# Expert stage of a two-layer fp32 kernel: stationary expert weights taken from a copy made by ScalarE, with the routing slots, two norms and the final sums rearranged

## The chip, the cores and the metric

The kernel runs on one core of a Trainium2 chip. The time is device microseconds (us) of that core for one execution; three runs of the kernel before took 1727.71, 1731.00 and 1731.02 us, so the median is 1731.0 us. One more execution was recorded by the hardware profiler. Engines are named as in the profile: PE is TensorE's matmul side, PEld its weight loads, DVE VectorE, ACT ScalarE, POOL GpSimd, SP the engine that issues most DMAs.

## The reference, cut to what matters

The program is two transformer layers over 4 x 512 tokens of width 256, all in float32. Layer 0 is a decayed linear attention and a gated feed-forward with Hadamard rotations. Layer 1 is an attention with 16 heads, then a second attention with 32 query and 8 key heads of width 64, and behind it a mixture of 16 experts of which each token takes 4. The change is mostly in the mixture:

```python
x = x + o @ wo
h = _rms(x, ff_ln_w)
logits = h @ wg
topv, topi = jax.lax.top_k(logits, TOP_K)
gate = jax.nn.softmax(topv, -1)
weights = jnp.zeros_like(logits).at[bidx, sidx, topi].set(gate)
a = jax.nn.silu(jnp.einsum('bsd,edh->bseh', h, w1)) * jnp.einsum('bsd,edh->bseh', h, w3)
y = jnp.einsum('bseh,ehd->bsed', a, w2)
moe = jnp.einsum('bsed,bse->bsd', y, weights)
return x + moe
```

Here d and h are both 256. The kernel computes only the four chosen experts of each token.

## The kernel before, in words

The kernel is written in stages, and in the stages spoken of here the order of work on each engine is the order of the program text (`manual_schedule`): each engine takes its instructions in that order, and waits on semaphores where data or a buffer is not ready. "Tile n" below is a group of 128 token rows of one expert.

**Layer 0 attention** (lines 657 to 685) walks over 16 groups of 128 tokens, and puts three or so pieces of the next batch's projections (`pieces_of`) into each step.

**Second attention of layer 1** (lines 1859 to 1950) walks over 16 units u, each in five slots f. Beside the attention itself, each slot calls `extras`, which takes pieces from three lists: the norms, and the routing of the batch before. `route(b)` is the routing of batch b, some 20 pieces and 16 scatters: squares, root, scale, the logits, the ranks of the 16 experts, gates, places in the experts' lists (`places`, 28 short matmuls), `choose` (the row numbers), and 16 scatters by POOL that write the tokens' rows into a DRAM list `xs`. After `route(2)` come `plan_tiles(0)` (four pieces) and `read_plan(0)`, which turn the counts into a list of tiles: for each of 79 tiles, where its rows start, where its expert's weights lie, how many rows are real. A call `extras(plain, banked, scatters)` lets that many pieces of each kind go; a "pause" ends a slot's plain pieces. `norms` (line 1081) makes the inverse deviations for the two norms in three pieces; its `begin` holds a DVE operation and the two ACT operations behind it.

**Expert stage** (lines 1955 to 2114). 79 tiles of 128 rows; the first 33 (`NFIRST`) need only the first three batches. `route(3)` and the second plan run inside this stage, two pieces an iteration. The weights of the experts in use lie in SBUF as `wall`, 1536 columns an expert (w1 and w3 in halves of the inner dimension, 1024 columns, then w2 in 512), fetched by 16 DMAs of 768 KB; a matmul finds its expert by a register address (`w_at`). For tile i:

- `fetch_rows(i)`: one DMA of 128 rows from `xs` into `xin`.
- `turn_in(i)`: two PE transposes of `xin` into PSUM (`ptx`), DVE copies them to `hTx`; three small DVE operations make the gate and the row numbers to which the tile goes (`goes`).
- `hidden(i)`: two matmuls with `hTx` stationary and 512 columns of `wall` moving, so that rows lie on partitions: `ph`. ACT makes `gx` = silu of the first half, DVE multiplies by the second half: `ax`.
- `turn_hidden(i)`: two PE transposes of `ax` into PSUM (`pa`), ACT copies them to `aTx`.
- `give(i)`: two matmuls with `aTx` stationary and 256 columns of `wall` moving: `pyx`. ACT scales by the gate (`yx`), and POOL adds the rows to one of two DRAM accumulators by an indirect DMA (`acc`, even tiles to one, odd tiles to the other).

A float32 matmul shows as two instructions on PE, so `hidden` is four of 512 columns and `give` four of 256. Line 1986 is the helper that issues both, so they are told apart by tile names. Iteration n of the loop holds, in this order: `hidden(n+1)`, the weights' DMA for place n+2, `address(n+2)`, `turn_in(n+2)`, `turn_hidden(n)`, `give(n-1)`, `fetch_rows(n+3)`, and two pieces of routing.

**End** (lines 2097 to 2114). For each batch, SP reads both accumulators, DVE adds them and the residual `xt`, and SP writes the result. Tile 78, the last, adds to the even accumulator.

## Time and profile before

| What | Value |
|---|---|
| median of three runs | 1731.0 us |
| profiled execution: its own time | 1726.86 us |
| profiled execution: span of the page | 1725.1 us |
| mean granted PE clock | 0.963 of full |
| PE, PEld busy | 1620.5 us (94%), 941.9 us (55%) |
| DVE, ACT, POOL busy | 1028.1, 825.9, 897.1 us |
| DMA over the span | 146.23 MB, 79 GB/s from and to HBM |
| second attention, by its first and last output projection | 733 to 1408 us |
| first transpose of a tile's rows, last `yx` | 1414.5 us, 1698.5 us |

A line of the profile's timeline gives the start in us, the length in us, the engine, the line of the kernel, the operation, the tile written and the tiles read, and in brackets how long the engine had been idle and what released it. Lines of a table by stretches give, for PE, PEld, DVE, ACT and POOL, the busy us and in brackets the number of instructions, then the granted PE clock (1.00 is full), the DMA engines' share and GB/s. Ends of matmuls are modelled; starts are recorded, so the pace of PE is read from starts.

### The profile page before, as it was taken

The page shows a single profiled execution, that of the slowest core. Times are in us where ns is not written, and L with a number is a line of the kernel's source. Part 1 is how long each engine was busy: PE and PEld are TensorE (multiplying, and loading weights), DVE is VectorE, ACT ScalarE, POOL GpSimd, SP SyncE. Part 2 cuts the span into 40 slices and gives each one's busy share as a digit, 9 for nine tenths or more (in the row PEclk, how much of TensorE's full clock was granted, in tenths as well). Part 3 has the DMA queues.
Part 4 walks back from the last instruction along what each step waited for, and adds up shares of the span by engine and source line. Part 5 has one row for each costly group of instructions (what it writes and reads, how often), then busy time and mean ns, then how long its engine had stood idle before and what let it go on. Part 6 is the DMA issues. An engine that isn't in the chain of part 4 may idle for free.

```text
span 1725.1 us, 36698 instructions
## 1 busy us (share of the span) xinstructions
PE 1620.5 (94%) x13412; PEld 941.9 (55%) x13412; DVE 1028.1 (60%) x3097; ACT 825.9 (48%) x2170; POOL 897.1 (52%) x914
## 2 busy tenths in 40 slices
PE   7999999999999999999999999999998878899993
PEld 4665554653333334566666666666665655555551
DVE  4556336556665621877777788778877734433333
ACT  4431122125655476666666666666664434333331
POOL 4224124206555477657476747894784415754442
PEclk9999999999998999899999999999998788999997
DMA  9993000001000010322212122322231138655556
GB/s 346 371 370 120 1 1 0 1 3 53 1 1 1 1 23 23 103 59 56 63 52 69 50 57 52 103 69 58 65 84 39 56 130 239 154 88 87 89 85 170
DMA packets 106913, 146.23 MB, mean 85 GB/s; under 512 B 11633, under 2 KB 86129, under 8 KB 106353
## 3 DMA queue, kind: packets, MB, share of 16 engines
q1 hardware_dynamic: 91856, 123.54, 23.2%
q0 software_dynamic: 14448, 19.80, 6.7%
q8 instruction: 109, 1.79, 0.4%
q14 instruction: 68, 0.55, 0.1%
q10 hardware_dynamic: 432, 0.55, 0.1%
HBM read 67.17 MB, written 68.29 MB: 79 GB/s over the span
## 4 chain that ended last, share of the span: by engine, by line
PE 75%; DVE 10%; ACT 7%; issue 3%; POOL 2%; DMA 1%; SPq 0%; DVEq 0%; ACTq 0%; POOLq 0%
PE ph L1986 9%; PE po L1428 8%; PE pgu L225 7%; PE sc L1355 6%; PE pr L225 6%; PE py L234 6%; PE py L1477 5%; PE sT L1164 5%; PE sc L329 4%; PE pyx L1986 4%; PE oT L1177 3%; ACT masked L1385 3%; PE pv L234 2%; DVE masked L1373 2%; PE pq L225 2%
## 5 line engine op out<-in xcount | busy, mean ns | idle before, releaser
L1385 ACT ACTIVATE masked<-masked,mx 128x512 f32<-128x512 f32 (+3 forms) x512 | 281.0, 553 | 15.6 <-DVE mx L1373 15.5
L1405 DVE STREAM_TRANSPOSE pT<-masked 128x512 f32<-128x512 f32 (+3 forms) x512 | 229.9, 489 | 51.5 <-ACT masked L1385 47.5
L1373 DVE CUSTOM_DVE_ANT_0 masked<-sc,cst 128x512 f32<-128x512 f32 (+3 forms) x512 | 213.8, 480 | 2.8 <-PE sc L1355 2.8
L335 DVE TENSOR_REDUCE top<-sc 128x1 f32<-128x512 f32 x256 | 158.8, 682 | 59.9 <-PE sc L329 59.9
L2068 POOL DMA_INDIRECT acc<-yx,goes x79 | 123.4, 1563 | 133.1 <-ACT yx L2067 98.2
L1355 PE MATMUL sc<-kr,qr 32*128 32x256 f32 (+3 forms) x2048 | 182.8, 457 | 10.1 <-DVE mx L1373 9.2
L1428 PE MATMUL po<-pT,vsr 32*64 32x256 f32 (+1 forms) x5376 | 171.6, 353 | 9.2 <-ACT h L989 2.9
L1986 PE MATMUL ph<-wall,hTx 128*128 x316 | 162.4, 638 | 8.0 <-DVE hTx L2024 7.5
L1428 PEld LDWEIGHTS po<-pT,vsr 32*64 32x64 f32 x5376 | 137.5, 135 | 52.2 <-issue 18.3
L1170 ACT ACTIVATE pT<-sT 128x512 f32<-128x512 f32 x256 | 131.8, 602 | 59.1 <-PE sT L1164 59.1
L1355 PEld LDWEIGHTS sc<-kr,qr 32*128 32x128 f32 x2048 | 98.8, 187 | 67.0 <-issue 26.3
L1477 PE MATMUL py<-wo,rsb 128*128 128x256 f32 x512 | 134.3, 409 | 0.0
L2048 DVE TENSOR_TENSOR ax<-ph,gx 128x256 f32<-128x256 f32 x79 | 33.5, 425 | 160.2 <-ACT gx L2046 160.1
L1486 POOL TENSOR_TENSOR z<-z,y 128x256 f32<-128x256 f32 x64 | 46.7, 729 | 155.0 <-ACT y L1485 153.9
L225 PE MATMUL pr<-hT,wq 128*128 128x512 f32 x256 | 123.5, 605 | 3.1 <-ACT h L989 2.6
L1012 POOL TENSOR_TENSOR part<-raw,rtab 128x512 f32<-128x512 f32 x80 | 103.2, 1291 | 32.0 <-ACT raw L1003 28.5
L1477 PEld LDWEIGHTS py<-wo,rsb 128*128 128x128 f32 x512 | 97.3, 200 | 38.7 <-ACT masked L1385 9.9
L225 PE MATMUL pgu<-xnT,wug 128*128 128x512 f32 x256 | 114.5, 598 | 1.5 <-DVE xnT L190 1.5
L1164 PE MATMUL sT<-qr,km 32*128 32x512 f32 x512 | 109.7, 645 | 6.4 <-DVE top L335 3.5
L1006 POOL TENSOR_TENSOR qr<-raw,rtab 128x512 f32<-128x512 f32 x64 | 81.8, 1299 | 52.7 <-ACT raw L1003 52.7
L1485 ACT COPY y<-py 128x256 f32<-128x256 f32 x64 | 23.6, 369 | 171.3 <-PE py L1477 171.2
L1385 ACT ACTIVATION_READ_ACCUMULATOR masked<-masked,mx 128x1 f32 x512 | 97.6, 191 | 0.0
(306 smaller groups left out, 2812.8 us busy)
## 6 DMA issues: line engine op xcount, KB each, us to landing
xs<-zero SPq DMA_DIRECT2D x16, 2304.0 KB, 20.0
vsr<-vd SPq DMA_DIRECT2D x256, 64.0 KB, 2.2
wall<-in_w_exp_dram SPq DMA_DIRECT2D x16, 768.0 KB, 5.6
xin<-xs SPq DMA_DIRECT2D x79, 144.0 KB, 2.2
wq<-in_w_q_dram SPq DMA_DIRECT2D x33, 256.0 KB, 2.8
kr<-krq SPq DMA_DIRECT2D x32, 256.0 KB, 4.2
acc<-zero SPq DMA_DIRECT2D x2, 2176.0 KB, 18.5
vd<-vs SPq DMA_DIRECT2D x64, 64.0 KB, 2.1
```

What stands on the lines that cost most here:

```text
L225: nc.tensor.matmul(dst, lhsT=w[:, c, cols], rhs=srcT[:, c, tok], start=(c == 0), stop=(c == n - 1),)
L234: nc.tensor.matmul(dst, lhsT=srcT[:, i, tok], rhs=w[:, c, cols], start=(i == 0), stop=(i == len(chunks) - 1),)
L335: nc.vector.tensor_reduce(top[:, at : at + 1], sc, AX.X, ALU.max)
L1164: nc.tensor.matmul(us[g], lhsT=km[rows(g), tok(c)], rhs=qr[rows(g), :], start=True, stop=True,)
L1170: nc.scalar.activation(pT[:, g, :], us[g], AF.Exp)
L1355: nc.tensor.matmul(scs[s][:, at : at + w], lhsT=qrs[2 * u + jj][rows(s), ab, tok(t)], rhs=krs[u][rows(s), ab, :w], start=(ab == 0), stop=( ...
L1373: nc.vector.tensor_tensor_reduce(masked[:, part], sc[:, part], C("cmask")[:, S - (t + 1) * P :], 1.0, 3e38, ALU.add, ALU.min, mx[:, t, i : ...
L1385: nc.scalar.activation(part, part, AF.Exp, bias=lots[u, "mx"][:, t, i : i + 1], scale=-1.0, accum_out=lots[u, "sm"][:, t, i : i + 1],)
L1405: nc.vector.transpose(turned[u, h][s % 2][:, 2 * jj + s // 2, to : to + w], p[:, at : at + w],)
L1428: nc.tensor.matmul(heaps[u, h][a][64 * g : 64 * g + 64, first * P : 2 * P], lhsT=vsrs[u][rows(a), c, 64 * g : 64 * g + 64], rhs=src, start ...
L1477: nc.tensor.matmul(py[:, :D], lhsT=oT[:, t % 2 * 4 + j, :], rhs=wo4[:, 4 * (u % 4) + j, :], start=(j == 0), stop=(j == 3),)
L1986: ins = nc.tensor.matmul(out, lhsT=lhsT, rhs=wall[:, bass.ds(w_at[i] + at, n)], **kw)
```

## The change

Five things, in the order of the diff.

1. In layer 0's attention, the third piece of the first step of a batch (the keys of the next batch) is put behind the output projection of the batch before.
2. `norms` comes in five pieces: the two ACT operations are split off from the DVE operation (`power`). Where the pieces run in the second attention, they are joined again in pairs.
3. In the second attention, the plain pieces let go in slots f = 0 to 4 are 2, 1, 2, 2, 0 for u up to 12 and 4, 1, 2, 2, 1 after it (before: 1, 1, 2, 2, 1, and 3 in each). In slots 0 and 4, three evictions instead of two go ahead of the exponentials.
4. In the expert stage, `fresh_weights(i)` has ACT copy the 1024 columns of w1 and w3 out of `wall` at the register address into one of two `ws` tiles. `hidden` has 128 x 128 blocks of `ws` stationary and `hTx` moving: eight matmuls of 128 columns (16 instructions on PE), and the inner features lie on partitions. So the product with the gate half is `aTx` itself; `turn_hidden`, its transposes and its ACT copy are gone, and `give(n)` comes an iteration earlier.
5. At the end, token p x 16 + i of the accumulators belongs to partition p (the row numbers `ids` are renumbered), so that a partition reads its four rows as one piece. The accumulator that is complete first is read first and gets the residual; the other is read in five parts, added and written.

```diff
-                for piece in more[1:]:
+
+                waits = more[2:] if t == 0 else []
+                for piece in more[1 : len(more) - len(waits)]:
                     piece()
...
                 if b > 0:
                     out0(b - 1, t)
+                for piece in waits:
+                    piece()
...
             nc.vector.tensor_scalar(st["v"], var, 1.0, eps, ALU.mult, ALU.add)
+
+        def power():
             st["y"] = stat.tile([P, n * NT], F32, tag="rn_y", name="rn_y")
...
-            lambda: begin(mvs[:, part, 1], EPS_LN),
-            second,
+            lambda: begin(mvs[:, part, 1], EPS_LN), power,
+            second, power,
...
-        for piece in norms(2, 2):
+        begin, power, second, again, end = norms(2, 2)
+        for piece in (lambda: (begin(), power()), lambda: (second(), again()), end):
...
-                for i in ("..0123", ".0.12.3", "..ww.0123", "..w.0.1.23", "..0123")[f]:
+                for i in ("...0123", ".0.12.3", "..ww.0123", "..w.0.1.23", "...0123")[f]:
...
             extras(
-                3 if u > 12 else 2 if f in (2, 3) else 1, 1 if f in (2, 3) else 0,
+
+                ((2, 1, 2, 2, 0), (4, 1, 2, 2, 1))[u > 12][f],
+                1 if f in (2, 3) else 0,
                 4 if u > 13 else 2,
             )
...
             w_at[i] = nc.values_load(
-                wats[0:1, i : i + 1], engines=[mybir.EngineType.PE],
+                wats[0:1, i : i + 1],
+                engines=[mybir.EngineType.PE, mybir.EngineType.Activation],
                 skip_runtime_bounds_check_because="a place times its width",
             )
+
+        def fresh_weights(i):
+
+            ws_[i] = ep.tile([P, 4 * D], F32, tag="ws", name="ws")
+            used(i, nc.scalar.copy(ws_[i], wall[:, bass.ds(w_at[i], 4 * D)]))
...
-            ph = pse.tile([P, 512], F32, tag="ph", bufs=2, name="ph")
-            for c in range(2):
-                matmul_expert(
-                    i, ph, hTs_[i][:, c, :], 2 * c * D, 2 * D,
-                    start=(c == 0), stop=(c == 1),
-                )
-            g = ep.tile([P, D], F32, tag="gx", name="gx")
-            nc.scalar.activation(g, ph[:, :D], AF.Silu)
-            a = ep.tile([P, D], F32, tag="ax", name="ax")
-            nc.vector.tensor_tensor(a, ph[:, D:], g, ALU.mult)
-            pas[i] = a
-
-        def turn_hidden(i):
...
+            ph = pse.tile([P, 4, P], F32, tag="ph", bufs=2, name="ph")
+            for m in range(4):
+                for c in range(2):
+                    at = 2 * c * D + m * P
+                    nc.tensor.matmul(
+                        ph[:, m, :], lhsT=ws_[i][:, at : at + P], rhs=hTs_[i][:, c, :],
+                        start=(c == 0), stop=(c == 1),
+                    )
+            g = ep.tile([P, 2, P], F32, tag="gx", name="gx")
+            nc.scalar.activation(g, ph[:, :2, :], AF.Silu)
             aTs[i] = ep.tile([P, 2, P], F32, tag="aTx", name="aTx")
-            nc.scalar.copy(aTs[i], pt)
+            nc.vector.tensor_tensor(aTs[i], ph[:, 2:, :], g, ALU.mult)
...
-        for n in range(-2, NSLOT + 1):
+        for n in range(-2, NSLOT):
             if 0 <= n + 1 < NSLOT:
                 hidden(n + 1)
-                if n + 2 < NEXP:
-                    fetch_weights(n + 2)
             if 0 <= n + 2 < NSLOT:
                 address(n + 2)
                 turn_in(n + 2)
             if 0 <= n < NSLOT:
-                turn_hidden(n)
-            if 0 <= n - 1 < NSLOT:
-                give(n - 1)
+                give(n)
+            if 0 <= n + 2 < NSLOT:
+                fresh_weights(n + 2)
+                if n + 3 < NEXP:
+                    fetch_weights(n + 3)
             if 3 <= n + 3 < NSLOT:
                 fetch_rows(n + 3)
...
+        late = (NSLOT - 1) % 2
+        parts = [(b, 0, NT) for b in range(B - 1)] + [(B - 1, 0, 2), (B - 1, 2, 2)]
         for b in range(B):
...
+            rows_in(1 - late, b, 0, NT)
+        for part in parts:
+            rows_in(late, *part)
         for b in range(B):
...
+                row = sums[1 - late, b][:, t, :]
+                nc.vector.tensor_tensor(row, row, xt[b * NT + t], ALU.add)
+        for b, t, n in parts:
+            both = sums[late, b][:, t : t + n, :]
+            nc.vector.tensor_tensor(
+                both, both, sums[1 - late, b][:, t : t + n, :], ALU.add
+            )
...
-        "ids": np.arange(B * S, dtype=np.int32).reshape(B * NT, P).T,
+        "ids": np.arange(B * S, dtype=np.int32).reshape(P, B * NT),
```

More of the change, by code (lines that the diff above doesn't have):

```diff
@@ L1968 @@
         units.append((pse, 2))
-        xin, hTs_, aTs, pas, gates_, w_at = ({} for _ in range(6))
+        xin, hTs_, aTs, ws_, gates_, w_at = ({} for _ in range(6))
         wp = w4.enter_context(tc.tile_pool(name="w_exp", bufs=1))
@@ L1983, in fetch_weights, with used @@
             tc.declare_no_dep(ins.ins, group="uses", reason="of places read before")
-        def matmul_expert(i, out, lhsT, at, n, **kw):
-            ins = nc.tensor.matmul(
-                out, lhsT=lhsT, rhs=wall[:, bass.ds(w_at[i] + at, n)], **kw
-            )
+        def used(i, ins):
             if i < NEXP:
@@ L2038, in hidden @@
         def hidden(i):
-            ph = pse.tile([P, 512], F32, tag="ph", bufs=2, name="ph")
-            for c in range(2):
-                matmul_expert(
-                    i, ph, hTs_[i][:, c, :], 2 * c * D, 2 * D,
-                    start=(c == 0), stop=(c == 1),
-                )
-            g = ep.tile([P, D], F32, tag="gx", name="gx")
-            nc.scalar.activation(g, ph[:, :D], AF.Silu)
-            a = ep.tile([P, D], F32, tag="ax", name="ax")
-            nc.vector.tensor_tensor(a, ph[:, D:], g, ALU.mult)
-            pas[i] = a
-        def turn_hidden(i):
-            pt = pse.tile([P, 512], F32, tag="pa", name="pa")
-            pt = pt[:, : 2 * P].rearrange("p (c n) -> p c n", c=2)
-            for c in range(2):
-                nc.tensor.transpose(pt[:, c, :], pas[i][:, c * P : (c + 1) * P], ident)
+            ph = pse.tile([P, 4, P], F32, tag="ph", bufs=2, name="ph")
[8 more added lines that the diff above has]
+            nc.scalar.activation(g, ph[:, :2, :], AF.Silu)
             aTs[i] = ep.tile([P, 2, P], F32, tag="aTx", name="aTx")
-            nc.scalar.copy(aTs[i], pt)
+            nc.vector.tensor_tensor(aTs[i], ph[:, 2:, :], g, ALU.mult)
         def give(i):
@@ L2061, in give @@
             for c in range(2):
-                matmul_expert(
-                    i, py, aTs[i][:, c, :], (4 + c) * D, D,
+                used(i, nc.tensor.matmul(
+                    py, lhsT=aTs[i][:, c, :],
+                    rhs=wall[:, bass.ds(w_at[i] + (4 + c) * D, D)],
                     start=(c == 0), stop=(c == 1),
-                )
+                ))
             y = ep.tile([P, D], F32, tag="yx", bufs=4, name="yx")
@@ L2098, with rows_in @@
         sums = {}
-        for b in range(B):
-            for i, acc in enumerate(accs):
-                sums[b, i] = sp.tile([P, NT, D], F32, tag=f"sum{b}{i}", name="sum")
-                nc.sync.dma_start(
-                    out=sums[b, i],
-                    in_=acc[b * S : (b + 1) * S, :].rearrange("(t p) d -> p t d", p=P),
-                )
+        def rows_in(i, b, t, n):
+            if (i, b) not in sums:
+                sums[i, b] = sp.tile([P, NT, D], F32, tag=f"sum{b}{i}", name="sum")
+            nc.sync.dma_start(
+                out=sums[i, b][:, t : t + n, :],
+                in_=accs[i][: B * S, :].rearrange("(p i) d -> p i d", p=P)[
+                    :, b * NT + t : b * NT + t + n, :
+                ],
+            )
+        late = (NSLOT - 1) % 2
+        parts = [(b, 0, NT) for b in range(B - 1)] + [(B - 1, 0, 2), (B - 1, 2, 2)]
+        for b in range(B):
+            rows_in(1 - late, b, 0, NT)
+        for part in parts:
+            rows_in(late, *part)
         for b in range(B):
-            nc.vector.tensor_tensor(sums[b, 0], sums[b, 0], sums[b, 1], ALU.add)
             for t in range(NT):
-                nc.vector.tensor_tensor(
-                    sums[b, 0][:, t, :], sums[b, 0][:, t, :], xt[b * NT + t], ALU.add
-                )
+                row = sums[1 - late, b][:, t, :]
[4 more added lines that the diff above has]
+                both, both, sums[1 - late, b][:, t : t + n, :], ALU.add
+            )
             nc.sync.dma_start(
-                out=out[b].rearrange("(t p) d -> p t d", p=P), in_=sums[b, 0]
+                out=out[b].rearrange("(t p) d -> p t d", p=P)[:, t : t + n, :], in_=both
             )
```

## The prediction, made before the changed kernel was run

> **What bounds the kernel now.** I read the page's busy shares first, then the timeline of one tile in the expert stage, the waits there, and the chain's last pieces. PE is busy 94% of the span, but this doesn't say what a tile costs. The timeline of one tile does:
>
> ```profile
> 1601.03 0.30 PEld L1986 LDWEIGHTS ph<-wall,hTx 128*128 128x128 f32 x2 [0.36 <-DVE hTx L2024]
> 1601.04 1.98 PE L1986 MATMUL ph<-wall,hTx 128*128 x4
> 1602.86 0.38 PE L2022 MATMUL ptx<-ident,xin 128*128 128x128 f32 x2
> 1603.06 0.38 ACT L2046 ACTIVATE gx<-ph 128x256 f32<-128x256 f32 x1 [1.47 <-PE ph L1986]
> 1603.08 0.38 PE L2055 MATMUL pa<-ident,ax 128*128 128x128 f32 x2
> 1603.29 1.03 PE L1986 MATMUL pyx<-wall,aTx 128*128 x4
> 1603.47 0.42 DVE L2048 TENSOR_TENSOR ax<-ph,gx 128x256 f32<-128x256 f32 x1 [2.02 <-ACT gx L2046]
> 1603.81 0.42 DVE L2024 COPY hTx<-ptx 128x256 f32<-128x256 f32 x1
> 1604.28 0.30 PEld L1986 LDWEIGHTS ph<-wall,hTx 128*128 128x128 f32 x2 [0.36 <-DVE hTx L2024]
> 1604.36 0.47 ACT L2067 ACTIVATE yx<-pyx,gate 128x256 f32<-128x256 f32 x1 [0.44 <-PE pyx L1986]
> ```
>
> A tile takes 1604.28 - 1601.03 = 3.25 us. Starts give the parts: `hidden` 1.83 (four passes of 0.43 and 0.11 until the first weights are in), `turn_in` 0.22, `turn_hidden` 0.21, `give` 0.99. The last holds some 0.1 of waiting: the next `hidden` waits for `hTx`, which stands on DVE behind `ax`, which waits for `gx`. So PE and this ring of ACT and DVE are balanced. ACT is mostly idle. `yx` begins 1.07 us after the first pass of `give` (1604.36 - 1603.29), when PE has **already begun** the next `hidden`; nothing on PE waits for `yx`.
>
> **The expert tile, part by part.** Out go two transposes (0.21 us of PE) and the ACT copy `aTx` (0.37). `hidden` becomes 16 passes of 128 columns, each with its own 128 x 128 load. The nearest row has that shape, the state update of layer 0 (times in us):
>
> ```profile
> 66.94 0.53 PEld L542 LDWEIGHTS pkv<-vz,kd 128*128 128x128 f32 x4
> 67.05 0.61 PE L542 MATMUL pkv<-vz,kd 128*128 128x128 f32 x4
> ```
>
> Four loads of 0.19 end 0.53 after the first began: one every (0.53 - 0.19) / 3 = 0.113, loads beside passes. So 16 x 0.113 = 1.81, with the first load 1.92 against 1.83. Here a rule speaks against the change. The Trainium skill, "TensorE: Matmul & The Clock Gate", under "The mechanism", says that a weight load overlaps a running matmul only where their row groups differ; these use all rows. By the rule a pass would cost load plus pass, some 0.11 + 0.11, and `hidden` 3.5 us, 1.6 more a tile. I take the row, and keep the rule as a rival. PE's own work is then 1.92 + 0.22 + 0.86 (four passes of 0.215) = 3.00 us.
>
> **The copy** is new. Nearest row, an ACT copy from SBUF of half the width:
>
> ```profile
> L1444 ACT COPY wide<-rs x8: 612/617/631, 1318.5 to 1391.0; 128x512 f32<-128x512 f32 x8
> ```
>
> ACT evictions of 256 and 512 columns take 372 and 586 ns, so 0.836 ns a column; 617 + 512 x 0.836 = 1.045 us. Between 0.9 (the slope alone) and 1.3 (two copies of 617) I take 1.05. ACT would be busy 0.38 + 0.47 + 1.05 = 1.90 us a tile, which fits in 3 us. But **where it stands in ACT's queue decides**. ACT's order in iteration n is `gx(n+1)`, `yx(n)`, copy(n+2). `yx(n)` waits for the end of `give(n)`, PE's last work in the iteration; PE's next is `hidden(n+2)`, whose stationary operand is copy(n+2). So PE waits through `yx` and the copy in every tile. From the first load of `hidden`: `give` begins at 1.92 + 0.22 = 2.14; `yx` at 2.14 + 1.07 = 3.21; it ends at 3.68; the copy, begun up to 0.1 before `yx` ends as ACT's neighbours do, ends at 4.63 to 4.73; the next load 0.05 later (PE follows ACT by that in the trace). **Period 4.68 to 4.78, I take 4.75, against 3.25.** Behind the waiting load stand `turn_in` and `give`, hence the next `yx` and POOL's accumulation, so everything takes this pace. The ACT register load of `address` (0.30 on PE's side now) lies between `gx`, over at 2.5, and `yx` at 3.21; without that cover it would cost 0.3 a tile. DVE's ring ends at 2.5 + 0.42 + 0.42 = 3.3, inside the period. SP's weight DMAs go out one place further ahead, its row fetches as before, both slower than now; nothing there is late.
>
> **The clock.** PE would idle about 1.55 us in each 4.75, as the profile counts idle. In this trace the clock changes only on a grid of 3.413 us, and falls to half after a stretch of that grid with little PE work:
>
> ```profile
> 1429.87:1433.28 3.41, 1.35 (x3) 0.68 (x4) 1.19 (x5) 1.84 (x4) 1.28 (x2) 1.00 0.36 143
> 1433.28:1436.70 3.42, 3.42 (x10) 2.33 (x9) 1.19 (x5) 0.76 (x2) 3.06 (x8) 0.50 0.82 203
> 1501.54:1504.95 3.41, 1.73 (x4) 0.42 (x3) 0.58 (x2) 0.38 (x1) 2.72 (x6) 1.00 0.69 72
> 1504.95:1508.36 3.41, 1.30 (x8) 1.01 (x8) 0.79 (x4) 0.37 (x1) 3.07 (x2) 1.00 0.99 282
> 1508.36:1511.77 3.41, 3.41 (x6) 1.50 (x5) 0.06 (x1) 0.47 (x1) 1.55 (x1) 0.50 0.59 99
> ```
>
> The first number after the width is PE's busy time, the third from the end the clock. After 1.35 and 1.30 us the next stretch is at half, after 1.73 it is not. The same page, under "Why this matters for your kernels", asks for no PE gaps over about 3 us; by it a gap of 1.55 is far from harm. The row's margin is thinner: the worst stretch would hold 3.41 - 1.55 = 1.86 us of PE. Both say that the clock stays, so nothing is added; the thin margin is a rival.
>
> **The sum over the expert stage.** `hidden` begins for tiles 0, 5, 22 and 78 at 1415.81, 1442.46, 1508.63 and 1691.98.
> - Tiles 22 to 78: 56 x 4.75 = 266.0 against 183.35: **+82.7**.
> - Tiles 5 to 22: 17 x 4.75 = 80.8 against 66.2. Of the 3.1 us of short matmuls in `places`, half fits into PE's gap; with the slow stretch that follows them now too, and one table load, I add 3.4: **+18**. (The 3.79 us for which PE waits for rows at 1507 mostly disappears in the slower pace; that is in it.)
> - Tiles 0 to 5: 5.33 us each now, at half clock part of the time and with four table loads of 1.28. The copies come on top where those loads stand ahead of `gx`: **+3.5**, between 0 and 8.
>
> **Routing slots.** Counting the lists through for both versions: `choose` of batch 2 moves from u = 15, f = 0 to f = 4, its last four scatters from u = 15, f = 3 to the slot with f = 2 behind the last unit, `read_plan` from u = 15, f = 3 to the slot with f = 1 behind it. Now POOL is done with scatters long before the attention ends:
>
> ```profile
> 1386.87 0.96 POOL L1664 DMA_INDIRECT xs<-hx,ati  x1 [0.19 <-issue]
> 1408.69 0.72 POOL L1486 TENSOR_TENSOR z<-z,y 128x256 f32<-128x256 f32 x1 [1.00 <-ACT y L1485]
> 1409.44 0.39 SPq L1980 DMA_DIRECT2D wall<-in_w_exp_dram  x1
> ```
>
> The first weights wait for the last `z` on POOL (memory of the attention's tiles), the first rows for the scatters. After the change, `choose` ends at about 1392, 16 scatters at 1.28 (0.96, a memset, a gap) take 20.5, four `z` among them 3: the last `z` ends near 1417.5 instead of 1409.4. Bounds 0 and +10; **+8**. Against this, DVE's four plan pieces move to where DVE is idle for 7.4 us (1394.7 to 1402.0), and the rank pieces stand farther from their transposes (PE waited 2.9 us for an eviction `h` at 1280): between -10 and +6, **-4**. The split norms give ACT's Ln less to wait for or more; its queue waited 15.7 us there, none of which PE shows: 0.
>
> **Layer 0.** PE waits 3.2 us in all for `xnT` ahead of the keys; an output projection of 0.9 fits in twice: **-1.5**.
>
> **The end.** Now:
>
> ```profile
> 1700.22 3.65 DMA acc<-yx,goes
> 1709.39 8.92 DMA sum<-acc
> ```
>
> The last accumulation lands at 1703.87, 11.9 us after tile 78's `hidden` began; eight reads (4 MB) land by 1718.3, 14.4 us later, then 6.8 of adds and writing. After: last `yx` ends near 4.6, POOL's 1.55 and landing put it at about 9; the first accumulator's reads start near 7. At the same rate all is read at 21.6, and 5 more for a half part's add and write: 27 against 33.1. **-6**; if only the order counts and not the longer runs of memory, -4.
>
> Sum: 82.7 + 18 + 3.5 + 8 - 4 - 1.5 - 6 = **+100.7**. The profiled execution took 1726.9, 4.1 below the median of the runs shown; 1731.0 + 100.7 = **1832**.
>
> **Rivals.**
> - *Faster: the copy is hidden.* It needs nothing of tile n; its buffer is free after `hidden(n)`. If it ran in ACT's idle 1.47 us, before `yx`, PE's 3.00 would set the pace: 73 tiles at -0.25 are -18, with the other terms (8 - 4 - 1.5 - 6) -22: 1709. It decides once the copy begins no later than 1.95 after `hidden` begins, so that it ends with `give`; as written it can't before 3.6. Against it: `gx`, `aTx`, `yx` come in the text's order in the tiles I looked at. 7%.
> - *The clock falls.* If a third of the stretches fell to half, each costing some 1.4 us of PE time: 78 x 4.75 / 3.41 / 3 x 1.4 = +51, 1883; every other one, 1910. For it: the margin of 0.1 to 0.5 us, sampled at all phases. 15%.
> - *Loads don't overlap*: 78 x 1.6 = +125, 1957. Against it the row above. 4%.
> - *Part of the wait is saved* (copy begun early behind `yx`, shorter than reckoned; period 4.35): -29, 1803. 8%.
> - Main case: 66%, own range 1812 to 1862.
>
> **Range and chances.** A measurement of this kernel tells 0.2% (3.5 us) from no change. 1800 to 1890 holds nearly all of the main case, most of the shorter wait, and the clock's milder half. Faster 0.06, same 0.01, slower 0.93.
>
> **What would show it.** Right: tiles at 4.7 apart; PEld for `ph` waiting for ACT `ws` some 1.6 us in nearly every tile; copies near 1.05, right behind `yx`; clock 1.00 between; `ph` loads every 0.113; last `z` and first `wall` DMA near 1417; the last add of the end 6 us nearer to the last accumulation. Wrong: copies ahead of `yx`, clock rows of 0.5 through the stage, or loads every 0.22.

## The result, and the profile after

The changed kernel took **1779.5 us** (median of four executions, 1776.4 to 1784.5), beside 1729.4 us for the kernel before on the same chip (now four executions): a ratio of **1.030**, 95% interval 1.026 to 1.034. It is slower, as predicted, but by 50 us and not by 101: 1779.5 lies below the range of 1800 to 1890. The profiled execution took 1782.08 us with a span of 1780.2, which is 55.1 above the span before; its mean PE clock rose from 0.963 to 0.978.

The timeline of one tile of the steady part, after (start, duration, engine and line, operation, output and inputs; in brackets the idle time ahead of it and what ended that; lines between these, of weight loads, DVE, POOL and SP, are left out):

```profile
1653.08 1.86 PEld L2056 LDWEIGHTS ph<-hTx,ws 128*128 128x128 f32 x16 [1.90 <-ACT ws L2028]
1653.08 2.05 PE L2056 MATMUL ph<-hTx,ws 128*128 128x128 f32 x16 [1.50 <-ACT ws L2028]
1654.97 0.38 PE L2034 MATMUL ptx<-ident,xin 128*128 128x128 f32 x2
1655.17 0.38 ACT L2061 ACTIVATE gx<-ph 128x256 f32<-128x256 f32 x1 [2.14 <-PE ph L2056]
1655.19 1.03 PE L2068 MATMUL pyx<-wall,aTx 128*128 x4
1656.26 0.47 ACT L2074 ACTIVATE yx<-pyx,gate 128x256 f32<-128x256 f32 x1 [0.70 <-PE pyx L2068]
1656.63 1.03 ACT L2028 COPY ws<-wall 128x1024 f32 x1
...
1657.71 0.97 PEld L2056 LDWEIGHTS ph<-hTx,ws 128*128 128x128 f32 x8 [1.90 <-ACT ws L2028]
```

A tile takes 1657.71 - 1653.08 = 4.63 us. The copy stands right behind `yx`, takes 1.03, and the next load begins 0.05 after its end. PE has waited 1.50 and its weight side 1.90 by then. In the page's list of costliest groups the same wait, over all 79 tiles:

```profile
L2056 PEld LDWEIGHTS ph<-hTx,ws 128*128 128x128 f32 x1264 | 151.6, 196 | 147.0 <-ACT ws L2028 147.0
```

So the mechanism is the predicted one. The missing 46 us lie elsewhere. Marks that both traces have cut the program into stages (layer 0's attention ends with the first `ph` behind it; the end of a unit of the second attention is the first of the two `rsb` copies by ACT that stand 1 us apart):

| Stage | predicted | measured, from the two traces |
|---|---|---|
| layer 0's attention | -1.5 | -1.6 (157.6 to 156.0) |
| first attention of layer 1, with the split norms | 0 | **-14.8** (the second attention's first mask at 695.5, 679.1) |
| second attention, units 0 to 12 | not in the sum | -3.2 (end of unit 12 at 1228.0, 1208.5) |
| units 13 to 15, with the routing slots | -4 | **-31.4** (154.0 to 122.6) |
| from there to the first `hidden` | +8 | +11.9 (33.8 to 45.7) |
| tiles 0 to 5 | +3.5 | +1.5 (26.65 to 28.19) |
| tiles 5 to 22 | +18 | +18.1 (66.2 to 84.2) |
| tiles 22 to 78 | +82.7 | +77.8 (183.35 to 261.1) |
| from tile 78's `hidden` to the end | -6 | -3.3 (33.1 to 29.8) |
| sum | +100.7 | +55.1 |

Three rows are to be read with care, as the traces of all fourteen kernels show. The layer 0 part was never run alone, and its mark lies anywhere from 155.4 to 160.7 in the eight kernels without it and from 153.5 to 156.6 in the six with it. The stage of units 0 to 12 takes from 526.5 to 532.6 us, so its 3.2 can't be told from scatter. And of the 3.3 at the end, 2.6 come with the new loop: with that loop and the old end, tile 78's `hidden` stands 30.5 us from the end.

Two terms that I had set at nothing or next to it bring 42 of the 46 us. Both lie in stages where PE looked busy. The stretches tell how. First attention of layer 1, before, from 500 us to the second attention's first mask (span in us, then busy time and instructions of PE, PEld, DVE, ACT and POOL, then the granted PE clock, DMA share, GB/s):

```profile
500.00:695.50 195.50, 188.00 (x1048) 72.92 (x1044) 89.14 (x188) 113.55 (x224) 119.44 (x103) 0.95 0.05 13
```

Units 13 to 15 of the second attention, before:

```profile
1228.00:1382.00 154.00, 139.84 (x1652) 93.44 (x1650) 111.95 (x399) 80.94 (x259) 95.01 (x131) 0.88 0.20 59
```

and after:

```profile
1208.50:1331.10 122.60, 119.55 (x1624) 80.93 (x1623) 100.27 (x343) 81.11 (x258) 80.77 (x103) 1.00 0.23 64
```

PE's idle time in the three units falls from 14.2 to 3.1 us. Its busy time falls too, by 20.3, for nearly the same number of matmuls: the clock was at half for stretches of 37.5 us in all before, and never after. If work takes twice its time at half clock, half of 37.5 was extra, 18.8, close to those 20.3. So 11.1 us less waiting went with 31.4 us less time: the slow work behind the waits cost more than the waits.

The larger waits that PE had there, before (what waited, on whom, us in all, times, longest):

```profile
PE sc L1355 <- DVE mx L1373: 6.5, 2, 3.3
PE po L1428 <- ACT h L989: 2.9, 1, 2.9
PE po L1428 <- ACT lg L1558: 2.2, 1, 2.2
PE pt L983 <- POOL hn L1526: 1.2, 2, 0.8
```

and after:

```profile
PE sc L1361 <- DVE mx L1379: 2.0, 1, 2.0
PE sc L1361 <- POOL qr L1017: 0.3, 1, 0.3
PE po L1434 <- ACT h L993: 0.3, 1, 0.3
```

`lg` and `hn` belong to the routing, and `h` is ACT's eviction of the routing's transposes. The waits for `lg` and `hn` are gone after; that for `h` is nearly gone. The largest, for `mx`, stands behind routing pieces on DVE too. In the timeline before, three rank pieces hold DVE from 1310.3 to 1315.7 ahead of the wait that ends at 1319.26, and plan pieces from 1364.0 to 1370.7 ahead of the one that ends at 1374.18. After, one wait of 2.0 for `mx` is left.

### The profile page after: what moved, and what is told of

It reads as the page before. It is cut to its first block, busy times and chain, and to the rows that moved or that the text cites. A ratio compares the mean times of both kernels' runs of the same rounds, so it can differ in the third digit from the quotient of the medians.

```text
span 1780.2 us, 38207 instructions
## 1 busy us (share of the span) xinstructions
PE 1582.0 (89%) x14202; PEld 998.2 (56%) x14202; DVE 1021.2 (57%) x3098; ACT 871.8 (49%) x2170; POOL 895.5 (50%) x914
## 4 chain that ended last, share of the span: by engine, by line
PE 67%; DVE 10%; ACT 10%; issue 6%; POOL 5%; DMA 2%; SPq 0%; ACTq 0%; DVEq 0%; POOLq 0%
PE sc L1361 7%; PE ph L2056 7%; PE po L1434 7%; PE pgu L225 6%; PE pr L225 6%; PE py L234 5%; PE py L1483 5%; PE sT L1170 5%; PE sc L329 3%; ACT ws L2028 3%; PE oT L1183 3%; PE pv L234 2%; ACT masked L1391 2%; PE pq L225 2%; POOL acc L2075 1%
## 5 line engine op out<-in xcount | busy, mean ns | idle before, releaser
L2056 PE MATMUL ph<-hTx,ws 128*128 128x128 f32 x1264 | 166.8, 287 | 116.4 <-ACT ws L2028 113.9
L2056 PEld LDWEIGHTS ph<-hTx,ws 128*128 128x128 f32 x1264 | 151.6, 196 | 147.0 <-ACT ws L2028 147.0
L1361 PE MATMUL sc<-kr,qr 32*128 32x256 f32 (+3 forms) x2048 | 178.8, 456 | 7.0 <-DVE mx L1379 5.8
L2063 DVE TENSOR_TENSOR aTx<-ph,gx 128x256 f32<-128x256 f32 x79 | 33.6, 425 | 260.6 <-ACT gx L2061 260.6
L1434 PE MATMUL po<-pT,vsr 32*64 32x256 f32 (+1 forms) x5376 | 165.7, 342 | 3.0 <-ACT raw L1007 1.7
L1483 PE MATMUL py<-wo,rsb 128*128 128x256 f32 x512 | 128.3, 395 | 3.0 <-DVE rsb L1474 3.0
L1361 PEld LDWEIGHTS sc<-kr,qr 32*128 32x128 f32 x2048 | 95.2, 187 | 61.9 <-issue 27.0
L1492 POOL TENSOR_TENSOR z<-z,y 128x256 f32<-128x256 f32 x64 | 46.7, 730 | 133.0 <-ACT y L1491 132.9
L2061 ACT ACTIVATE gx<-ph 128x256 f32<-128x256 f32 x79 | 30.3, 384 | 167.0 <-PE ph L2056 167.0
## 6 DMA issues: line engine op xcount, KB each, us to landing
xs<-zero SPq DMA_DIRECT2D x16, 2304.0 KB, 19.5
```

Of the source, the lines that this page charges most:

```text
L1361: nc.tensor.matmul(scs[s][:, at : at + w], lhsT=qrs[2 * u + jj][rows(s), ab, tok(t)], rhs=krs[u][rows(s), ab, :w], start=(ab == 0), stop=( ...
L1434: nc.tensor.matmul(heaps[u, h][a][64 * g : 64 * g + 64, first * P : 2 * P], lhsT=vsrs[u][rows(a), c, 64 * g : 64 * g + 64], rhs=src, start ...
L1483: nc.tensor.matmul(py[:, :D], lhsT=oT[:, t % 2 * 4 + j, :], rhs=wo4[:, 4 * (u % 4) + j, :], start=(j == 0), stop=(j == 3),)
L2056: nc.tensor.matmul(ph[:, m, :], lhsT=ws_[i][:, at : at + P], rhs=hTs_[i][:, c, :], start=(c == 0), stop=(c == 1),)
```

## The experiments

Ratios are against the kernel before on the same chip, with a 95% interval; three chips served, on which the kernel before took 1731.4, 1731.7 and 1747.4 us. Where an expectation below gives a time for a run on the third (empty pieces, counts, order), 16 us are to be added to it. Positions in time come from one profiled execution of each kernel.

### One part of the change alone

**The split norms alone.** The kernel before, with the norms' part of the diff:

```diff
             nc.vector.tensor_scalar(st["v"], var, 1.0, eps, ALU.mult, ALU.add)
+
+        def power():
             st["y"] = stat.tile([P, n * NT], F32, tag="rn_y", name="rn_y")
...
-            lambda: begin(mvs[:, part, 1], EPS_LN),
-            second,
+            lambda: begin(mvs[:, part, 1], EPS_LN), power,
+            second, power,
...
```

> The kernel before with the split norms alone (the DVE operation and ACT's Ln and Exp as pieces of their own in layer 1's first attention; nothing else). Theory A (ACT's Ln stands behind a DVE operation of the same step, up to 4.7 us, PE runs out of work behind ACT, and the clock falls to half for one to three stretches of 3.41 us): 15 us less, near 1714, with no half-clock stretches between 525 and 605 us. Theory B (the 15 us of that stage come from something else in the change): no difference, 1729.

Measured: 1719.1 us, ratio 0.9915 (0.9885 to 0.9946): A, at 12 us in place of 15, and no stretch of half clock from 525 to 605. This is the first big miss of my sum.

**The slots alone.** The kernel before, with the counts of pieces and the order of evictions:

```diff
-                for i in ("..0123", ".0.12.3", "..ww.0123", "..w.0.1.23", "..0123")[f]:
+                for i in ("...0123", ".0.12.3", "..ww.0123", "..w.0.1.23", "...0123")[f]:
...
-                3 if u > 12 else 2 if f in (2, 3) else 1, 1 if f in (2, 3) else 0,
+                ((2, 1, 2, 2, 0), (4, 1, 2, 2, 1))[u > 12][f],
+                1 if f in (2, 3) else 0,
```

> The kernel before with the slots of the second attention alone (numbers of pieces and the third eviction ahead of the exponentials). Theory A (the pieces stood too close together in u = 13 to 15, PE stalled and lost the clock): 29 to 33 us less in units 13 to 15, and some 7 us given back between the last projection and the first expert tile; near 1704. Theory B (the half-clock stretches of before in these units were a matter of the phase in which the stage meets the clock's grid, which the 16 us gained before the stage shift): less than 10 us gained, over 1720.

Measured: 1705.5 us, ratio 0.9838 (0.9805 to 0.9872): A. Units 13 to 15 take 122.4 us as in the changed kernel; the first attention keeps its half-clock stretches. From the end of unit 15 to the first `hidden` 46.2 us pass, 12 more than before, where A had 7.

**The expert loop alone.** The kernel before, with `fresh_weights`, the new `hidden` and the new order of the loop:

```diff
+        def fresh_weights(i):
+            ws_[i] = ep.tile([P, 4 * D], F32, tag="ws", name="ws")
+            used(i, nc.scalar.copy(ws_[i], wall[:, bass.ds(w_at[i], 4 * D)]))
...
```

> The kernel before with the expert loop alone changed (copy by ACT, 16 narrow passes, no second transposes; the old end). Theory A (PE waits in each tile through yx and the copy): tiles 4.64 apart, 97 us more, near 1826. Theory B (part of what the profile of the changed kernel shows as gained ahead of the expert stage is really the expert stage's doing): 50 us more, near 1780.

Measured: 1826.2 us, ratio 1.0561 (1.0514 to 1.0608): A. The loop alone costs 95 us, close to the 104 that I had for its tiles (82.7 + 18 + 3.5).

**The end alone.** The kernel before, with the renumbered `ids` and the new order of the sums:

```diff
-        "ids": np.arange(B * S, dtype=np.int32).reshape(B * NT, P).T,
+        "ids": np.arange(B * S, dtype=np.int32).reshape(P, B * NT),
...
```

> The kernel before with the end alone (renumbered rows, early accumulator read first with the residual). The prediction had 6 us less; the changed kernel's trace shows 3.3 from the last tile's start, in a loop whose last tiles stand differently. If the order of the reads counts: 4 to 6 us less, near 1724. If what counts is the landing of the last accumulation: 2 or less.

Measured: 1732.2 us, ratio 0.9998 (0.9976 to 1.0020): no gain that can be told, so the second figure (2 or less). From tile 78's `hidden` to the end its trace has 31.2 us, where the kernel before has 33.1. The chain in it shows a longer last accumulation:

```profile
1711.04 6.18 DMA acc<-yx,goes
```

In the kernel before this took 3.65. Now the early reads begin 1.2 us behind its issue. Where they begin 1.8 us or more behind it, as in the changed kernel, it takes 3.6 again. That the reads are the reason was not tried.

**All but the expert loop.** The changed kernel with the loop of before:

```diff
-                give(n)
-            if 0 <= n + 2 < NSLOT:
-                fresh_weights(n + 2)
+                turn_hidden(n)
+            if 0 <= n - 1 < NSLOT:
+                give(n - 1)
...
```

> The changed kernel with the expert loop of before (all other parts of the change kept). If the parts simply add: 1731 less 15 (norms), 27 (slots), 2 (layer 0) and 0 to 2 (end), near 1686; the expert loop then costs 94 to 96 us. If the parts share a cause (the same phase of the clock's grid), the sum falls short: over 1695.

Measured: 1686.5 us, ratio 0.9720 (0.9692 to 0.9748). The parts add up: 0.9915 x 0.9838 x 0.9998 = 0.975, and with the loop's 1.0561 the product is 1.030, the ratio of the whole change. Within these intervals, no part needs another one to work.

### Why the norms gain

Two causes fit the norms' gain: the ACT queue that no longer waits, or the mere shift of all later pieces by two places. To tell them apart, the two added pieces are left empty, and both ACT operations stay with their DVE operation:

```diff
+        def power():
+            pass
+
...
-            lambda: begin(mvs[:, part, 1], EPS_LN),
-            second,
+            lambda: begin(mvs[:, part, 1], EPS_LN), power,
+            second, power,
...
```

> The kernel before, with the norms of the first attention of layer 1 in five pieces as in the change, but the two ACT operations stay in one piece with the DVE operation, and the two added pieces are empty: every later piece moves by the same places as with the split norms alone, but ACT's Ln still stands right behind the DVE operation it waits for. Theory A (the gain of the split comes from ACT's queue no longer waiting for DVE, so that PE has no gap that costs the clock): the time stays near the kernel before, 1728 to 1734 us, and the stretches of half clock near 525 and 593 us remain. Theory B (the gain comes from where the later pieces stand): 1717 to 1722 us, as with the split alone.

Measured: ratio 0.9959 (0.9935 to 0.9983), 1740.8 us on a chip where the kernel before took 1747.4. By the total this lies between the two theories. The stage itself is clear. Its stretch from 500 us to the first mask, with empty pieces:

```profile
500.00:696.30 196.30, 188.84 (x1064) 71.06 (x1060) 87.79 (x189) 115.61 (x227) 121.19 (x104) 0.96 0.05 13
```

and with the split norms alone:

```profile
500.00:678.90 178.90, 174.82 (x1040) 66.75 (x1036) 86.43 (x187) 113.51 (x223) 118.44 (x103) 1.00 0.06 14
```

With empty pieces the stage ends at 696.3, as before (695.5), with the clock at 0.96; with the real split it ends at 678.9, with the clock at 1.00. So in this stage it is the wait, not the places: A. The other traces agree. All seven kernels without the split have 14 to 31 us of half clock between 500 and 650 us and take 537.6 to 543.3 us from the first `ph` to the first mask; all seven with it have none and take 521.1 to 526.7. Within each group the kernels differ in much else, and in where they meet the clock's grid, so this is not the luck of one trace. The 7 us that the empty pieces gained in the total come from somewhere else. I have no trace of the kernel before from that chip, so where they come from stays open.

The wait itself, ACT's Ln in the kernel before:

```profile
522.39 0.21 ACT L1089 ACTIVATE rn_y<-rn_v 128x4 f32<-128x4 f32 x1 [2.60 <-DVE rn_v L1087]
529.88 0.20 ACT L1089 ACTIVATE rn_y<-rn_v 128x4 f32<-128x4 f32 x1 [4.62 <-DVE rn_v L1087]
588.34 0.20 ACT L1089 ACTIVATE rn_y<-rn_v 128x4 f32<-128x4 f32 x1 [2.60 <-DVE rn_v L1087]
595.93 0.20 ACT L1089 ACTIVATE rn_y<-rn_v 128x4 f32<-128x4 f32 x1 [4.73 <-DVE rn_v L1087]
```

with the split norms:

```profile
522.20 0.21 ACT L1091 ACTIVATE rn_y<-rn_v 128x4 f32<-128x4 f32 x1
534.51 0.24 ACT L1091 ACTIVATE rn_y<-rn_v 128x4 f32<-128x4 f32 x1
578.77 0.21 ACT L1091 ACTIVATE rn_y<-rn_v 128x4 f32<-128x4 f32 x1
587.90 0.21 ACT L1091 ACTIVATE rn_y<-rn_v 128x4 f32<-128x4 f32 x1 [1.42 <-DVE rn_v L1087]
```

Behind a waiting Ln stand ACT's exponentials `pT` and its copy `raw`, and others wait for these. The timeline before has the way from the first Ln, over at 522.6, to PE:

```profile
524.65 0.61 ACT L1187 COPY raw<-oT 128x512 f32<-128x512 f32 x1
525.30 0.01 DVE L1189 LOAD_MASK_SELECT sums<-raw  x1 [2.94 <-ACT raw L1187]
526.64 1.12 PE L1164 MATMUL sT<-qr,km 32*128 32x512 f32 x2 [0.69 <-DVE top L335]
532.04 1.21 PE L329 MATMUL sc<-kz,qp 32*128 32x512 f32 x1 [1.27 <-ACT pT L1170]
```

DVE waits 2.94 us for the late `raw`; its `top` stands behind that, and PE waits 0.69 for `top`. The last line is the wait for `pT` behind the second Ln, which ended at 529.88. PE's waits of these two kinds from 500 us to the first mask, before:

```profile
PE sT L1164 <- DVE top L335: 2.5, 4, 0.8
PE sc L329 <- ACT pT L1170: 1.9, 2, 1.3
```

With the split norms, 0.9 us are left of the first and nothing of the second. Before, the clock was at half for 10.2 us from 528.7, right behind the stretch that holds the wait of 0.69, and again for 3.4 us each at 552.6, 593.6 and 600.4: 20.4 us at half, none of it with the split.

### Which half of the slots gains

The counts of pieces alone, for units 13 to 15:

```diff
-                3 if u > 12 else 2 if f in (2, 3) else 1, 1 if f in (2, 3) else 0,
+                (4, 1, 2, 2, 1)[f] if u > 12 else 2 if f in (2, 3) else 1,
+                1 if f in (2, 3) else 0,
```

> The kernel before, with only the counts of routing pieces of the second attention changed for units 13 to 15 (4, 1, 2, 2, 1 in slots 0 to 4 in place of 3 in each); the order of evictions and exponentials and the counts of the earlier units stay. Theory A (fewer pieces in a slot keep PE from waiting for the routing's evictions, and keep the clock up): 1703 to 1710 us, nearly all of the gain of the counts and the order together. Theory B (the eviction that goes ahead of the exponentials in slots 0 and 4 is what counts): 1722 to 1731 us.

The order of the evictions alone:

```diff
-                for i in ("..0123", ".0.12.3", "..ww.0123", "..w.0.1.23", "..0123")[f]:
+                for i in ("...0123", ".0.12.3", "..ww.0123", "..w.0.1.23", "...0123")[f]:
```

> The kernel before, with only the order in slots 0 and 4 of the second attention changed (three evictions instead of two ahead of the exponentials); all counts stay. Theory A (the counts make the gain): within 4 us of the kernel before. Theory B (the order makes it): 1704 to 1712 us.

Measured: counts 0.9957 (0.9934 to 0.9980), order 0.9918 (0.9886 to 0.9950). With the 16 us added, the counts alone stand at the edge of theory B, and the order alone falls between its two theories: both halves gain, 7 and 14 us. Their product, 0.9875, is not far from the 0.9838 of both, which ran on another chip. In the traces of this chip units 13 to 15 take 169.0 us in the old form (the kernel with empty pieces), 142.0 with the counts, 158.2 with the order. But fewer pieces in the units leave more routing behind them: from the end of unit 15 to the first `gx` the counts take 54.4 us, where the order takes 39.1 and the kernel before 38.9. The order's gain is kept; over half of the counts' gain is handed back at the entrance to the expert stage. In the changed kernel, too, 11.9 of 31.4 go there.

### Where the copy stands

If the copy's place in ACT's queue sets the pace, moving it should move the pace. First **to the head of the iteration**, so that ACT's order is copy, `gx`, `yx`:

```diff
         for n in range(-2, NSLOT):
+            if 0 <= n + 2 < NSLOT:
+                address(n + 2)
+                fresh_weights(n + 2)
+                if n + 3 < NEXP:
+                    fetch_weights(n + 3)
             if 0 <= n + 1 < NSLOT:
                 hidden(n + 1)
             if 0 <= n + 2 < NSLOT:
-                address(n + 2)
                 turn_in(n + 2)
             if 0 <= n < NSLOT:
                 give(n)
-            if 0 <= n + 2 < NSLOT:
-                fresh_weights(n + 2)
-                if n + 3 < NEXP:
-                    fetch_weights(n + 3)
```

> The changed kernel with the copy moved to the head of the iteration, so that ACT's order is copy(n+2), gx(n+1), yx(n). Theory A (PE waited only because the copy stood behind yx; next in line is DVE's ring: hTx(n+2) stands behind aTx(n+1), which waits for gx at the end of the narrow passes, 3.3 us after a tile begins): tiles 3.3 apart, 103 us less than the changed kernel, near 1678. Theory B (the prediction's rival: with the copy hidden PE's own 3.0 us set the pace): 128 less, near 1653. Theory C (the copy itself loads ACT or SBUF so that its place matters little): over 1750.

Measured: 1700.9 us, ratio 0.9823 (0.9791 to 0.9854): faster than before, but 23 above A and far from B. Against the profile of the changed kernel (by the starts of `gx`), tiles 22 to 78 gain 70.5 us, at 3.38 a tile; A's 3.3 would give 75. Tiles 5 to 22 gain 17.8 (A: 23), tiles 0 to 5 nothing (A: 7). The profiled execution took 1691.3, which is besides 10 below the median. In the steady part PE now waits for something else:

```profile
PE ph L2056 <- DVE hTx L2036: 11.4, 42, 0.3
```

42 waits of 0.27 in the stretch of 140 us that this view covers: `hTx` stands on DVE behind `aTx`, which waits for `gx` of the same tile. That is the ring of the kernel before, still closed.

Then **between `gx` and `yx`** (the copy right behind `turn_in`):

```diff
                 address(n + 2)
                 turn_in(n + 2)
-            if 0 <= n < NSLOT:
-                give(n)
-            if 0 <= n + 2 < NSLOT:
                 fresh_weights(n + 2)
                 if n + 3 < NEXP:
                     fetch_weights(n + 3)
+            if 0 <= n < NSLOT:
+                give(n)
```

> The changed kernel with the copy between gx(n+1) and yx(n) in ACT's queue. Theory A (what counts is when ACT can begin the copy: at the end of gx, 2.45 after the tile's first load, so it ends at 3.5): tiles 3.55 apart, 85 us less than the changed kernel, near 1695. Theory C (its place matters little): over 1750.

Measured: 1727.5 us, ratio 0.9983 (0.9962 to 1.0004): 32 above A, and not C. Tiles come 3.84 apart, not 3.55. The same waits of PE's weight side as in the changed kernel, shorter:

```profile
PEld ph L2056 <- ACT ws L2028: 39.9, 36, 1.4
```

From a tile's first load, `gx` begins 2.09 later and takes 0.38; the copy begins 0.26 after that, takes 1.04, and the next load follows at 0.06: 3.83. The 0.26 between `gx` and the copy is idle time on ACT that the profile puts down to `gx` itself, which had ended. The register load of `address` stands there in ACT's queue; the prediction has it at 0.3 where nothing covers it, and 3.55 is without it. That it is the cause was not tried.

Last, **the ring opened**: the copy first, and `turn_in(n+2)` ahead of `hidden(n+1)`, so that DVE makes `hTx` before it waits for `gx`:

```diff
                 address(n + 2)
                 fresh_weights(n + 2)
+                turn_in(n + 2)
                 if n + 3 < NEXP:
                     fetch_weights(n + 3)
             if 0 <= n + 1 < NSLOT:
                 hidden(n + 1)
-            if 0 <= n + 2 < NSLOT:
-                turn_in(n + 2)
```

> As the kernel before this one in the list, and turn_in(n+2) ahead of hidden(n+1) as well, so that DVE makes hTx(n+2) before it waits for gx(n+1). Theory A (DVE's ring is next in line): tiles 3.0 apart, 25 us less than with the copy first alone, near 1655. Theory B (PE's work sets the pace already): no difference between the two.

Measured: **1663.0 us, ratio 0.9601 (0.9568 to 0.9634)**: A, 8 above its figure, and faster than both kernels. It stands 38 below the kernel with the copy first, where A had 25. Its timeline of one tile (PE's matmuls and some lines of ACT, DVE, POOL and SP are left out):

```profile
1541.02 1.86 PEld L2056 LDWEIGHTS ph<-hTx,ws 128*128 128x128 f32 x16
1541.33 0.42 DVE L2036 COPY hTx<-ptx 128x256 f32<-128x256 f32 x1 [0.24 <-PE ptx L2034]
1541.96 1.04 ACT L2028 COPY ws<-wall 128x1024 f32 x1 [0.37 <-ACT yx L2074]
1542.81 0.73 PEld L2068 LDWEIGHTS pyx<-wall,aTx 128*128 128x128 f32 x4
1543.57 0.36 PEld L2034 LDWEIGHTS ptx<-ident,xin 128*128 128x128 f32 x2
1543.89 0.41 PEld L2056 LDWEIGHTS ph<-hTx,ws 128*128 128x128 f32 x3
```

No load waits. The copy runs while PE is in `hidden`, and a tile takes 1543.89 - 1541.02 = 2.87: 1.79 for the 16 passes, 0.76 for `give`, 0.32 for `turn_in`. This is PE's own time. So with stationary weights a tile can take 0.38 us less than the 3.25 of the kernel before, once the copy and the ring are off PE's path. Beside the kernel with all but the expert loop, on the same chip, the loop in this form gains 23.5 us (1686.5 to 1663.0).

### How much wait the clock bears

The falling clock was the largest of my rivals, at 15%. To see how far off it was, the copy is widened to 1536 columns, of which the last 512 are not read:

```diff
-            ws_[i] = ep.tile([P, 4 * D], F32, tag="ws", name="ws")
-            used(i, nc.scalar.copy(ws_[i], wall[:, bass.ds(w_at[i], 4 * D)]))
+            ws_[i] = ep.tile([P, 6 * D], F32, tag="ws", name="ws")
+            used(i, nc.scalar.copy(ws_[i], wall[:, bass.ds(w_at[i], 6 * D)]))
```

> The changed kernel with the copy of ACT widened from 1024 to 1536 columns (the last 512 are not read): some 0.43 us more a copy, by 0.83 ns a column. Theory A (the copy stands whole on the path, and the clock bears PE's wait): tiles 5.06 to 5.08 us apart, 78 x 0.43 = 34 more, 1813 us, clock at 1.00 through the stage. Theory C (PE's idle of about 1.93 us a tile, which leaves 1.48 us of work in the worst stretch of 3.413 us, is past what the clock bears): stretches of half clock recur in the stage, and the time is 1830 us or more.

Measured: 1915.8 us, ratio 1.0963 (1.0920 to 1.1006): C. A's 1813 us would be 1813 / 1731 = 1.047. The copy takes 1.46 us, as reckoned, but tiles 22 to 78 come 6.30 apart on average. Stretches of the 3.413-us grid (width, PE's busy time and instructions, the other engines, then clock, DMA share, GB/s):

```profile
1701.68:1705.10 3.42, 1.50 (x11) 1.09 (x10) 0.52 (x4) 1.83 (x2) 1.54 (x1) 1.00 0.16 43
1705.10:1708.51 3.41, 3.41 (x16) 3.23 (x15) 0.90 (x4) 0.38 (x1) 0.00 (x0) 0.50 0.34 38
1708.51:1711.92 3.41, 1.49 (x11) 1.07 (x11) 0.29 (x2) 1.83 (x2) 1.54 (x1) 1.00 0.19 45
1711.92:1715.33 3.41, 3.41 (x16) 3.08 (x14) 1.07 (x5) 0.38 (x1) 0.00 (x0) 0.50 0.31 41
...
1735.81:1739.23 3.42, 1.54 (x13) 1.55 (x14) 0.00 (x0) 1.82 (x2) 1.54 (x1) 1.00 0.35 62
1739.23:1742.64 3.41, 1.59 (x11) 1.14 (x9) 1.19 (x5) 2.16 (x3) 1.03 (x1) 1.00 0.21 34
1742.64:1746.05 3.41, 3.13 (x22) 2.68 (x22) 0.80 (x4) 0.57 (x3) 0.51 (x1) 1.00 0.46 73
```

After 1.50 and 1.49 us of work the next stretch is at half; after 1.54 and 1.59 it is not. Between 1480 and 1880 us, 48 of the 50 full-clock stretches with up to 1.50 us of work were followed by half clock, and none of the 17 with 1.54 or more. Nearly all of the 50 are one pattern that repeats, at 1.49 or 1.50. While the clock stayed up, from 1737.68 to 1762.98, five tiles took 5.06 each, just A's figure. In the steady part of the changed kernel no stretch holds less than 1.68, and all but that one hold 1.91 or more. So 0.43 us more of waiting a tile would have made my rival of a falling clock the result.

## Why the prediction was right or wrong

**The expert tile: right.** The copy's place behind `yx` set the pace, as worked out. 4.64 us a tile against 4.68 to 4.78: `yx` began 3.18 after the first load (3.21 predicted), the copy begins 0.10 before `yx` ends, and takes 1.03 (1.05). For tiles 22 to 78 I had 266.0 and the trace has 261.1: 4.9 us too many, as 4.75 lay above what a tile takes. Tiles 5 to 22 met +18; tiles 0 to 5 came 2 below.

**Loads beside passes: right, and the rule too narrow.** The 16 loads of `hidden` take 1.86 us in all, one every (1.86 - 0.19) / 15 = 0.111, as the state update's row said (0.113). The Trainium skill, "TensorE: Matmul & The Clock Gate", under "The mechanism", has loads overlap running matmuls only where row groups differ; all of these use all rows, and they overlap. The same section also lets a load run ahead into a background weight buffer, and that sentence is the one that these rows agree with. By the narrower one the tile would have been 1.6 longer, by the prediction's estimate.

**The clock of the expert stage: right, with the margin about where I had put it.** The worst stretch in the steady part holds 1.68 us of PE's work and the others 1.91 or more, where I had 1.86 for the worst; no clock row of the steady part is below 1. But the rows that I read it from were too few: in the same trace the clock fell behind 2.63 to 2.77 us of work in the first attention. The skill page's advice of no PE gap over some 3 us ("Why this matters for your kernels") would let the wider copy pass, whose gaps on PE are 1.92; the measurement does not.

**The split norms: the step that failed first.** "The split norms give ACT's Ln less to wait for or more; its queue waited 15.7 us there, none of which PE shows: 0." PE did show it, one or two engines further on: it waited for `pT` and for `top` (1.9 and 2.5 us), which stood behind the Ln or behind what it delayed. I had looked for waits that name `rn_y`. The right question was what is queued behind the Ln on ACT, and who waits for that. And I had priced only idle time, not the half clock behind it. PE's idle time in the stage from 500 us on was 7.5 us and half of its half clock 10.2, 17.7 together. Measured: -14.8 (the part alone: -12 in the total).

**The routing slots: the step that failed worst.** "DVE's four plan pieces move to where DVE is idle [...] between -10 and +6, -4." I priced two single waits, behind the plan pieces (3.3 us for `mx`) and for `h` (2.9), at 4 together, and the clock behind them at nothing. I did not look at the whole of three units that had PE idle for 14.2 us and the clock at 0.88. Idle time of 14.2 and half of 37.5 us of half clock make 33 together. I had used the trace's clock rows to ask whether the new waits would lower the clock, but never to ask where the old ones had lowered it already. Measured -31.4, and with the entrance to the expert stage (+11.9 against +8) net -19.5, against +4 in my sum.

**Units 0 to 12** were not in the sum at all. Their 3.2 is within the scatter of that stage.

**The end: mechanism right, size off.** The term: "all is read at 21.6, and 5 more for a half part's add and write". The timeline after:

```profile
1757.77 5.29 SPq L2111 DMA_DIRECT2D sum<-acc  x9
1769.63 4.95 DVE L2130 TENSOR_TENSOR sum<-sum 128x1024 f32<-128x1024 f32 x5 [0.54 <-DMA sum<-acc]
1770.89 4.97 SPq L2133 DMA_DIRECT2D out_dram<-sum  x5
```

The late accumulator's first part is read at 1769.54, and its add begins 0.09 later. The next two parts land at 1770.81 and 1772.06, and their adds begin at 1770.90 and 1772.15, so adds do run between landings, as meant. The last half part lands at 1773.35, which is 23.0 behind tile 78's `hidden` (1750.38) in place of 21.6. From there to the end of the span it is 6.8 in place of 5: the last half add waits for the one ahead of it until 1773.9, and its write follows. Together 29.8 in place of 27.

**Rivals.** "The copy is hidden" I gave 1709, with PE's 3.00 us as the pace. Hidden copies do exist, and the runs price them: 3.38 us a tile while the DVE ring is closed, 2.87 when it is open. So that rival was wrong twice, and in both directions: it forgot the ring, and PE's own time was reckoned 0.13 too long. "Loads don't overlap" fell. "The clock falls" was 0.43 us of waiting a tile away.

## What to carry to other kernels

Price a wait on a helper engine by asking what is queued behind it and who waits for that, not by whether the bounding engine names it. Where the granted clock of a stage is below 1, count the idle time there and half of the half-clock stretches as what a change to that stage can win, before looking at its pieces: here 33 and 17.7 us, of which 31.4 and 14.8 came. An operand that is prepared by another engine belongs ahead of that engine's work for the current tile, and the engines' queues should then be followed once around for the next ring that closes: here moving a copy and a transpose turned 3% slower into 4% faster, of which 2.8% are the other parts of the change.

## What the runs showed of the hardware that was not expected

- In the expert stage, whose fp32 matmuls use the full array, the clock's border is narrow. On the grid of 3.413 us, half clock came behind 48 of 50 stretches with 1.50 us of PE work or less (by the profile's busy time), and behind none of 17 with 1.54 or more, though no gap of PE there was longer than 2.2 us. That is between 44 and 45% of the stretch. The two exceptions held as little as the rest, so busy time alone doesn't decide it.
- The border isn't the same for all work. In the first attention, whose matmuls `sT` and `sc` use 32 of the 128 rows, stretches with 2.63 to 2.77 us of PE work (from 525.3, 549.2, 590.1 and 597.0 before) were followed by half clock. That the rows in use are the reason was not tried.
- An indirect accumulation took 6.18 and 6.19 us from issue to landing in the two traces in which reads of the other accumulator began 1.1 to 1.2 us behind it (the end alone, all but the expert loop). It took 3.65 in the kernel before, where none ran beside it, and also in the changed kernel, where reads began 1.84 behind it.
- The same kernel before took 1731 us on two chips and 1747 on a third. There is no trace of it from the third chip, but the four other traces from there show PE waiting 4 to 9 times for nothing that the profile names, 1.9 to 5.0 us in all; the ten from other chips have two such waits, 1.3 us. Unit 13 of the second attention takes 46.3 to 46.7 us in those four and 40.9 to 41.1 in the ten. Why is open; parts of a change are to be compared on one chip.
